# Attention sums with 32-column products only, and a block's end in more steps

## The chip, the cores and the metric

The kernel runs on one core of one Trainium2 chip. The metric is device time in microseconds, from the launch of the one program to its end. TensorE is called PE here, VectorE DVE, ScalarE ACT, GpSimd POOL, SyncE SP.

## The reference, cut to what matters

One layer: graph attention over 4096 nodes with four heads, then a mixture of eight experts, two for each token. `adj` is a 4096 x 4096 int32 matrix of 0 and 1.

```python
h = jnp.einsum('nd,hdk->hnk', x, W)                     # 4 heads of 64 columns
s_col = jnp.einsum('hnk,hk->hn', h, a1)
s_row = jnp.einsum('hnk,hk->hn', h, a2)
e = leaky_relu(s_row[:, :, None] + s_col[:, None, :], 0.2)
e = jnp.where(adj[None] > 0, e, NEG_INF)
h_prime = jnp.einsum('hij,hjk->hik', softmax(e, -1), h)
out = jnp.transpose(h_prime, (1, 0, 2)).reshape(N, 256)
y = elu(out) + x @ Wr + br          # then a layer norm, and the sum with x
...
top_w, top_i = jax.lax.top_k(norm(x) @ Wg + bg, 2)      # 8 experts
out = out + w_dense[:, e:e+1] * (gelu(x @ W1[e] + b1[e]) @ W2[e] + b2[e])
```

All inputs are float32, and so are all products of the attention.

## The kernel before, in words

**Attention.** The adjacency comes transposed. The 4096 output rows are taken in four row blocks `a` of 1024 (`R`), each of two halves of 512 (`B`). For each row block, 32 column blocks `j` of 128 nodes pass by. For one j, DVE makes for each head h a tile `w` of 128 x 1024 weights (both halves) by one instruction (line 1235), from the row factors `er`, the column factor `eb` and the mask `am`. ACT makes the mask out of the int32 adjacency (line 1120), which SP loads. The pool of w has 10 tiles, four for a column block. PE then makes two kinds of products, both with the 512 elements of a w half as the moving operand:

- the rows (`sum_rows`, line 770): `ha` of a head, 64 columns, into `acc[half][h // 2]`, a PSUM bank for two heads. A product covers 64 of the 128 columns of PE's array; the products of heads 1 and 0, and those of heads 3 and 2, lie on different halves of the array and can run at the same time. Eight products for a column block.
- the weights' sums (`sum_weights`, line 779): `unit`, two columns, into two rows of `den` at partition 32 h. A product lies on one of four column groups of 32; the four heads can run at the same time. Eight products for a column block.

A float32 product appears in the profile as two matmuls and two weight loads. `attend` (line 785) makes rows first where j is even and in the last j, and sums first where j is odd, so that equal widths stand next to each other. `queue` (line 408) fixes the order of all these products among themselves. All else is placed between them by a scheduler, which orders the instructions of each engine when the kernel is built.

In the first row block, PE also projects the node features for coming column blocks (`norm_block`, `project_block`); there the first four column blocks are taken half by half.

**A row block's end.** `finish_blocks` (line 942) is a generator. Its first step copies the four accumulators and `den` to SBUF on ACT (lines 949, 952), which frees them for the next row block. Its other steps are run one by one, one after each column block of the next row block (in the last row block two after odd ones). They transpose `den` on PE (line 956) and take the reciprocals `z` on DVE; for each half (`finish_block`) they transpose the sums on PE (line 985, into `ptr`), scale them on ACT (line 987), and do ELU, residual, layer norm and the sum with x on DVE and ACT (lines 994 to 1014). `route_rows` (line 805) then transposes the normalised rows (line 815), multiplies with the router's weights in 32-column products (line 826), transposes the logits back (line 836), picks two experts for each token on DVE (lines 841 to 875), counts places by matmuls with a triangle and with ones (lines 884, 886), and writes the rows into the experts' lists by 16 indirect DMAs on POOL (line 934). For the first row block it also finds tokens that are not in a list (`missed`, `hit`, line 926). Each `yield` is a border between two steps. `ordered[0]` is false in this part and true after the attention.

**After the attention** come the expert tiles (`fetch`, `turn`, `up`, `down`), in an order written out by hand; the last row block's end runs among them (`sums_out`, `turn_sums`, `last_block`).

The general path (`with tc.If(general > 0)`), for scores of a wide spread, is not taken with these inputs.

## Time and profile before

| | us |
|---|---|
| median of 3 runs | 1320.18 |
| the runs | 1319.53 to 1321.72 |
| profiled execution | 1319.03 |
| its span | 1317.4 |
| row block 0 (with projection) | 29.7 to 275.1 |
| row block 1 | 275.1 to 457.7 |
| row block 2 | 457.7 to 639.6 |
| row block 3 | 639.6 to 821.7 |
| expert tiles | 821.7 to the end |

How to read it: the span is the time from the first to the last instruction that the profile shows; the profiled execution's time is 1.6 us longer, and the median of the runs is 1.2 us above that. In a line of a group or a timeline, "128\*64" means a product of 128 rows and 64 columns, "x2048" the number of instructions, "idle before" how long the engine had nothing to do, and "<-" what ended that. PE is the matmuls, PEld the weight loads. A matmul's duration contains its way through the array, so the distance from one start to the next, not the duration, tells the rate.

### The profile page before, as it was taken

The page shows a single profiled execution, that of the slowest core. Times are in us where ns is not written, and L with a number is a line of the kernel's source. Part 1 is how long each engine was busy: PE and PEld are TensorE (multiplying, and loading weights), DVE is VectorE, ACT ScalarE, POOL GpSimd, SP SyncE. Part 2 cuts the span into 40 slices and gives each one's busy share as a digit, 9 for nine tenths or more (in the row PEclk, how much of TensorE's full clock was granted, in tenths as well). Part 3 has the DMA queues.
Part 4 walks back from the last instruction along what each step waited for, and adds up shares of the span by engine and source line. Part 5 has one row for each costly group of instructions (what it writes and reads, how often), then busy time and mean ns, then how long its engine had stood idle before and what let it go on. Part 6 is the DMA issues. An engine that isn't in the chain of part 4 may idle for free.

```text
span 1317.4 us, 19120 instructions
## 1 busy us (share of the span) xinstructions
PE 1281.8 (97%) x7025; PEld 676.9 (51%) x7025; DVE 869.9 (66%) x1746; ACT 444.3 (34%) x888; POOL 226.7 (17%) x190
## 2 busy tenths in 40 slices
PE   7999999999999999999999999999999999999997
PEld 4423344222232222232222322888888877888886
DVE  6899977889999989999899997665111111121110
ACT  4212221135541336421355311533323332323332
POOL 1000010000006000015000150125222222222222
PEclk9999999999999999999999999999999999999999
DMA  7434333344444535535333341987866786878782
GB/s 220 173 97 160 101 108 97 112 149 119 118 128 149 172 90 136 144 101 157 97 112 100 101 153 42 331 265 206 281 164 194 185 185 150 194 207 209 177 213 51
DMA packets 144129, 202.43 MB, mean 154 GB/s; under 512 B 49712, under 2 KB 113856, under 8 KB 143376
## 3 DMA queue, kind: packets, MB, share of 16 engines
q1 hardware_dynamic: 122432, 161.26, 41.3%
q0 software_dynamic: 19360, 32.53, 11.0%
q10 hardware_dynamic: 2224, 7.22, 1.5%
q8 instruction: 60, 0.98, 0.3%
q14 instruction: 53, 0.43, 0.1%
HBM read 171.89 MB, written 29.08 MB: 153 GB/s over the span
## 4 chain that ended last, share of the span: by engine, by line
PE 58%; DVE 9%; issue 2%; ACT 1%; DMA 0%; POOLq 0%; DVEq 0%; ACTq 0%
PE po L1417 18%; PE ph L1386 17%; PE acc L770 14%; PE den L779 7%; DVE w L1235 6%; PE pt L1368 1%; DVE y L1014 0%; DVE y L1008 0%; DVE y L1000 0%; DMA out<-o_last,ids 0%; PE ptr L985 0%; PE pl L826 0%; DVE y L997 0%; PE ptx L815 0%; ACT y L987 0%
## 5 line engine op out<-in xcount | busy, mean ns | idle before, releaser
L1235 DVE SCALAR_TENSOR_TENSOR w<-er,eb,am 128x1024 f32<-128x1024 f32 x496 | 608.9, 1277 | 43.3 <-PE den L779 41.1
L770 PE MATMUL acc<-w,ha 128*64 128x512 f32 x2048 | 464.8, 599 | 7.5 <-DVE w L1235 7.0
L770 PEld LDWEIGHTS acc<-w,ha 128*64 128x64 f32 x2048 | 137.7, 137 | 303.5 <-issue 287.5
L1120 ACT ACTIVATE am<-adj 128x1024 bf16<-128x1024 int32 x124 | 131.1, 1057 | 373.5 <-DVE w L1235 323.0
L779 PE MATMUL den<-w,unit 128*2 128x512 f32 x2048 | 238.4, 594 | 7.5 <-DVE w L1235 7.1
L1386 PE MATMUL ph<-xT,w 128*128 128x256 f32 (+1 forms) x1056 | 240.8, 386 | 1.3 <-DVE xT L1372 0.7
L1417 PE MATMUL po<-w,hT 128*128 128x256 f32 x1088 | 240.3, 379 | 0.0
L1390 ACT ACTIVATE hT<-ph,bias 128x256 f32<-128x256 f32 (+1 forms) x264 | 126.5, 480 | 290.6 <-PE ph L1386 205.0
L1417 PEld LDWEIGHTS po<-w,hT 128*128 128x128 f32 x1088 | 205.5, 190 | 27.7
L1386 PEld LDWEIGHTS ph<-xT,w 128*128 128x128 f32 x1056 | 200.2, 190 | 35.8 <-DVE xT L1372 1.1
L1428 DVE SCALAR_TENSOR_TENSOR o<-po,share,b2s 128x256 f32<-128x256 f32 x66 | 31.8, 482 | 259.1 <-PE po L1417 246.2
L1439 POOL DMA_INDIRECT out<-o,ids x66 | 103.5, 1568 | 330.6 <-DMA out<-o,ids 205.1
L779 PEld LDWEIGHTS den<-w,unit 128*2 128x2 f32 x2048 | 43.9, 84 | 178.1 <-issue 151.7
L934 POOL DMA_INDIRECT lists<-xe,at x64 | 86.0, 1344 | 132.5 <-issue 55.0
L1018 POOL DMA_DIRECT2D out<-y x6 | 4.7, 782 | 335.6 <-issue 166.1
L1372 DVE COPY xT<-pt 128x256 f32<-128x256 f32 x13 | 5.5, 423 | 61.8 <-PE pt L1368 61.8
L188 ACT ACTIVATE m<-y,off 128x256 f32<-128x256 f32 x48 | 23.8, 499 | 23.3 <-DVE off L185 23.3
L1409 ACT ACTIVATE b2s<-b2b,share 128x256 f32<-128x256 f32 x68 | 30.8, 503 | 0.0
L626 PE MATMUL ph<-wall,xT 128*128 128x264 f32 x112 | 30.5, 392 | 0.3 <-DVE sc L636 0.3
L650 PE MATMUL pr<-wr,xT 128*128 128x256 f32 x112 | 29.5, 385 | 0.4 <-ACT xT L609 0.2
L987 ACT ACTIVATE y<-ptr,z 128x64 f32<-128x64 f32 x96 | 22.0, 312 | 15.3 <-PE ptr L985 15.3
L1235 DVE SCALAR_TENSOR_TENSOR w<-er,eb,er 128x512 f32<-128x512 f32 x32 | 22.1, 741 | 5.6 <-issue 5.1
(316 smaller groups left out, 620.0 us busy)
## 6 DMA issues: line engine op xcount, KB each, us to landing
w<-in_L_ffn_W SPq DMA_DIRECT2D x66, 1024.0 KB, 6.3
adj<-in_adj SPq DMA_DIRECT2D x126, 512.0 KB, 3.8
er<-parts ACTq DMA_DIRECT2D x3, 2048.0 KB, 7.7
b2b<-in_L_ffn_b SPq DMA_DIRECT2D x33, 128.0 KB, 3.6
early<-lists SPq DMA_DIRECT2D x16, 260.0 KB, 8.0
residual<-rb POOLq DMA_DIRECT2D x8, 512.0 KB, 3.8
rb<-residual SPq DMA_DIRECT2D x8, 512.0 KB, 4.4
out<-y POOLq DMA_DIRECT2D x8, 512.0 KB, 3.6
```

The source lines that it names most:

```text
L626: nc.tensor.matmul(ph, xT[:, c, ts(t, P)], wall[:, c, :], start=(c == 0), stop=(c == DC - 1),)
L770: queue(nc.tensor.matmul(acc[half][h // 2][ts(h % 2, K), :], ha[:, j, ts(h, K)], w[half][h], start=(j == 0), stop=(j == NT - 1),))
L779: queue(nc.tensor.matmul(den[h * Q : h * Q + HB, :], unit[:, j, h, 1 - half : 1 - half + HB], w[half][h], start=(j == 0 and half == 0), st ...
L934: ins = nc.gpsimd.indirect_dma_start(lists, bass.IndirectOffsetOnAxis(ap=at[:, k, t : t + 1], axis=0), xe[:, t, :], None,).ins
L1120: nc.scalar.activation(am, at, AF.Relu, scale=2.0)
L1235: nc.vector.scalar_tensor_tensor(wh[:, these], er[:, these, h], eb[:, j, h : h + 1], mask[:, these], op0=OP.max, op1=OP.min,)
L1386: order_of(nc.tensor.matmul(ph, job["w1"][:, c, ts(f, P)], xT[:, c, :], start=(c == 0), stop=(c == DC - 1),))
L1390: job["gelu"] = nc.scalar.activation(hT[:, f, :], ph, AF.Gelu, bias=job["bias"][:, f : f + 1]).ins
L1409: nc.scalar.activation(b2s[k], b2b, AF.Identity, scale=share[:, k : k + 1])
L1417: order_of(nc.tensor.matmul(po, hT[:, f, ts(k, CH)], w2[:, f, :], start=(f == 0), stop=(f == FC - 1)))
L1428: given_out.append(nc.vector.scalar_tensor_tensor(o, po, share[:, k : k + 1], b2s[k], op0=OP.mult, op1=OP.add).ins)
L1439: add()
```

## The change: what it does

1. **Every product of the attention lies on 32 columns.** A head's rows are made in two products of 32 columns each (`rows_of_head`), so a column block has 16 products of rows and 8 of sums. The sums of head h lie in `den` at 32 times `PLACE[h]`, where PLACE is (2, 3, 0, 1).
2. **`attend` mixes both kinds.** First the rows of heads 1 and 0, for each half; then for each half the sums of heads 1 and 0 with the rows of head 2; then for each half the rows of head 3 with the sums of heads 3 and 2. Each four in this order fills the four column groups. There is no longer a special order in the last column block.
3. **Two reciprocals for one** (`shares_of`), as heads no longer stand in order in `den`.
4. **More steps in `route_rows`**: before the transposes of the rows, between the router's products and the transposes of the logits, between these and what DVE takes of them, between the counting matmuls and what DVE takes of them; and, for the first row block, before and after the products of `hit`. With `ordered[0]` true the steps are as before.

```diff
+PLACE = (2, 3, 0, 1)
...
-        def sum_rows(w, j, halves):
+        def rows_of_head(w, j, half, h):
+
+            for g in range(K // Q):
+                here = h % 2 * K + g * Q
+                queue(nc.tensor.matmul(
+                    acc[half][h // 2][here : here + Q, :],
+                    ha[:, j, h * K + g * Q : h * K + (g + 1) * Q], w[half][h],
+                    start=(j == 0), stop=(j == NT - 1),
+                ))
+
+        def weights_of_head(w, j, half, h):
+
+            here = PLACE[h] * Q
+            queue(nc.tensor.matmul(
+                den[here : here + HB, :], unit[:, j, h, 1 - half : 1 - half + HB], w[half][h],
+                start=(j == 0 and half == 0), stop=(j == NT - 1 and half == HB - 1),
+            ))
+
+        def attend(w, j, halves):
+
 
             for half in halves:
-                for h in (1, 0, 3, 2):
-                    queue(nc.tensor.matmul(
-                        acc[half][h // 2][ts(h % 2, K), :], ha[:, j, ts(h, K)], w[half][h],
-                        start=(j == 0), stop=(j == NT - 1),
-                    ))
-
-        def sum_weights(w, j, halves):
-
+                for h in (1, 0):
+                    rows_of_head(w, j, half, h)
             for half in halves:
-                for h in reversed(range(H)):
-                    queue(nc.tensor.matmul(
-                        den[h * Q : h * Q + HB, :],
-                        unit[:, j, h, 1 - half : 1 - half + HB], w[half][h],
-                        start=(j == 0 and half == 0), stop=(j == NT - 1 and half == HB - 1),
-                    ))
-
-        def attend(w, j, halves):
-
-
-            rows_first = j % 2 == 0 or j == NT - 1
-            for add in (sum_rows, sum_weights) if rows_first else (sum_weights, sum_rows):
-                add(w, j, halves)
+                for h in (1, 0):
+                    weights_of_head(w, j, half, h)
+                rows_of_head(w, j, half, 2)
+            for half in halves:
+                rows_of_head(w, j, half, 3)
+                for h in (3, 2):
+                    weights_of_head(w, j, half, h)
+
+        def shares_of(pd):
+
+            z = small.tile([P, TB, H, HB], F32, tag="z", name="z")
+            for h in range(0, H, 2):
+                nc.vector.reciprocal(z[:, :, h : h + 2], pd[:, :, PLACE[h] : PLACE[h] + 2, :HB])
+            return z
...
             turned_rows = []
+            if not ordered[0]:
+                yield
             for g in range(0, n, TB):
...
                 nc.scalar.copy(lTs[-1], pl)
-            if ordered[0]:
-                yield
+            yield
             pg = bank([P, n, Q], "pg")
...
+            if not ordered[0]:
+                yield
             full = [P, n, E]
...
+            if not ordered[0]:
+                yield
             rank = small.tile(full, F32, tag="rank", name="rank", bufs=2)
...
+                yield
                 for e in range(E):
...
+                yield
                 nc.vector.tensor_copy(others, po)
...
-            z = small.tile([P, TB, H, HB], F32, tag="z", name="z")
-            nc.vector.reciprocal(z, pd[:, :, :, :HB])
+            z = shares_of(pd)
```

The last replacement is made in `finish_blocks` and in `turn_sums`.

## The prediction

> **What bounds the kernel now.** I read the page first, then busy time by stage, the chain of waits in order of time, the timeline of one steady stretch, and the built order of both kernels. "Column block" means one j; I count them 0 to 127 through the four row blocks (32 each).
>
> ```profile
> PE 1281.8 (97%) x7025; PEld 676.9 (51%) x7025; DVE 869.9 (66%) x1746; ACT 444.3 (34%) x888; POOL 226.7 (17%) x190
> ...
> L770 PE MATMUL acc<-w,ha 128*64 128x512 f32 x2048 | 464.8, 599 | 7.5 <-DVE w L1235 7.0
> ...
> L779 PE MATMUL den<-w,unit 128*2 128x512 f32 x2048 | 238.4, 594 | 7.5 <-DVE w L1235 7.1
> ```
> The attention is 703 us of PE work. Each product is two matmul records (2048 for 1024 products).
>
> ```profile
> core 0: us, PE busy (x) PEld busy (x) DVE busy (x) ACT busy (x) POOL busy (x), PEclk, DMA share, GB/s
> 29.70:275.10 245.40, 238.84 (x1316) 92.30 (x1316) 215.32 (x397) 55.01 (x112) 11.32 (x15) 0.99 0.41 131
> 275.10:457.70 182.60, 179.08 (x1117) 50.71 (x1117) 172.21 (x232) 71.88 (x132) 28.28 (x20) 1.00 0.44 130
> 457.70:639.60 181.90, 178.89 (x1109) 50.70 (x1105) 171.45 (x226) 70.79 (x130) 29.22 (x20) 1.00 0.43 123
> 639.60:821.70 182.10, 178.90 (x1108) 51.66 (x1105) 168.14 (x250) 63.42 (x122) 22.86 (x18) 1.00 0.33 102
> ```
> These are the four row blocks. PE idles 3.0 to 3.5 us in each of the last three, DVE 10 to 14: PE bounds them, with DVE close behind. After 821.7 come the expert tiles, which the change leaves as they are but for one more reciprocal on DVE, busy there for 125 of 495 us.
>
> The chain in a steady stretch, and the same place in the timeline:
> ```profile
> 422.37 7.02 PE acc L770 x32
> 429.39 3.54 PE den L779 x32
> ```
> ```profile
> 428.36 0.14 PEld L770 LDWEIGHTS acc<-w,ha 128*64 128x64 f32 x2 [0.28 <-issue]
> ...
> 429.32 0.11 PEld L779 LDWEIGHTS den<-w,unit 128*2 128x2 f32 x8 [0.81 <-issue]
> ...
> 429.75 0.10 PEld L779 LDWEIGHTS den<-w,unit 128*2 128x2 f32 x4 [0.33 <-issue]
> ...
> 432.86 0.20 PEld L770 LDWEIGHTS acc<-w,ha 128*64 128x64 f32 x4 [0.86 <-issue]
> ```
> A slot (loads of one pass of 2 wide or 4 narrow products) lasts 0.429 us, whether two products of 64 columns run in it or four of 2. Where the width changes, the load comes late (0.81 and 0.86 idle, not 0.3).
>
> **The change, part by part.**
>
> *Width changes, removed.* Two column blocks are 32 matmuls of rows at two a slot and 32 of `den` at four, 16 + 8 slots: 24 x 0.429 = 10.30 us, but the chain has 7.02 + 3.54 = 10.56. The 0.26 are the two width changes. After, a column block is 24 products in six fours, again 12 slots, with no change of width. 120 changes survive beside other work in the trace of before, so 60 pairs x 0.265 = 15.9 us less. The first slot of 64 columns after any whole-array work is about 0.05 longer too (433.35 against 432.86, 0.49, in the same timeline); some 27 such returns: 1.3 us less.
>
> Does a mix of 2 and 32 columns keep the rate? The router's products show it:
> ```profile
> 383.86 0.11 PEld L779 LDWEIGHTS den<-w,unit 128*2 128x2 f32 x4 [0.32 <-issue]
> 384.29 0.13 PEld L826 LDWEIGHTS pl<-xT,wg 128*32 128x32 f32 x4 [0.32 <-issue]
> 384.71 1.06 PE L826 MATMUL pl<-xT,wg 128*32 128x128 f32 x32
> ```
> From 2 to 32 columns costs nothing (384.29 - 383.86 = 0.43, idle 0.32 as inside a stretch). Thirty-two matmuls of 128 elements, four at a time, run 1.06 us with the tail of the last, 0.27: about 0.109 a slot. Four of these are 0.436, 0.007 over 0.429; as 512 elements pay a slot's fixed part once and not four times, I take 0.429 and keep 0.436 as the upper end: 12 x 128 x 0.007 = 10.8 us more. Lower end: 0.429, nothing gained, since the stream itself is as long.
>
> *Instructions.* 2048 matmul records and as many loads more; 96 instructions in a block's 5.15 us, 54 ns each. In the router's burst 64 went out in some 2.4 us after a wait of PE's own sequencer at 383.0, 38 ns each, so I cost the issue at nothing. [...]
>
> *Fours that are cut apart, added.* Each product holds one of four column groups for two slots, 0.858 us. In the built order of before, whole-array transposes stand between whole pairs or fours everywhere. In the changed one many stand after 7 of 24 products (four of the first half, three of the second, then the transposes, then the eighth): seven products take 2 x 0.858, the other 17 take 5 x 0.858, seven turns for six. Counting, between whole-array instructions, the fullest column group against a quarter of the products, I get 6 extra turns in row block 0 (blocks 8 to 23; one more in the start-up, hidden), 3 in the next (36, 42, 43), 4 (67, 68, 74, 75), 5 (98, 99, 103, 104, and 111 to 113): 18 x 0.858 = 15.4 us more. Bounds: 0 if PE waits there anyway, 15.4 if it never does. I take all, as DVE has its idle time just there (2.4 us before 280.6, 2.3 before 303.6).
>
> *PE's waits for DVE.* In odd blocks `den` comes first and needs all four w tiles at once:
> ```profile
> 315.19 1.04 PE L779 MATMUL den<-w,unit 128*2 128x512 f32 x8 [1.02 <-DVE w L1235]
> ...
> 362.42 1.90 PE L779 MATMUL den<-w,unit 128*2 128x512 f32 x16 [1.13 <-DVE w L1235]
> ```
> After, heads 1 and 0 suffice to begin; head 2 is due 1.7 us later, head 3 3.4. Heads 0 and 1 are also given back a third of a block earlier, so DVE gets ahead further. A tile takes DVE 1.20 (chain), four 4.80, under PE's 5.15. Such waits are 2.4 us in row block 1, as much in 2 (the same places), 1.4 in 3; with PE faster some stay: I take 4.5 of 6.2 away, bounds 0 and 6.2. The hit matmuls' wait (0.5 us, once) goes with the new step behind the comparisons: 5.0 together.
>
> *Block's end.* At j = 31 the rows used to come before `den`, which left four slots to empty the accumulators. Now the last rows and `den` end together, and the next block needs `den` empty after four slots, not eight. In the built order of ACT the copy of `den` stands behind one more mask at row blocks 2 and 3:
> ```profile
> 457.90 0.69 ACT L952 ACTIVATE ud<-den,tiny 128x512 f32<-128x512 f32 x1 [0.27 <-PE den L779]
> 460.33 1.06 ACT L1120 ACTIVATE am<-adj 128x1024 bf16<-128x1024 int32 x1 [1.75 <-DVE w L1235]
> ```
> That mask waits for DVE's last w of two blocks on: with h0 and h1 back 1.5 us before the end, two tiles of 1.20 and the mask of 1.06, `den` is copied (0.69) at about 2.9 after the end, where PE wants it at 1.72: 1.2 lost, twice. Queued behind: the next masks, which have a block's lead. Row block 1 loses 0.3 (its copies wait for the sums already). Together 2.6 more; bounds 0 and 4.
>
> *Steps and reciprocals.* Four more steps per row block, six in the first: at one a block they end by block 58, 88 and 114, before the next row block; the list writes on POOL (some 25 us) start up to 18 us later but nobody waits until the first expert tile, whose rows are loaded at 797.6 and used at 821.6. Four more reciprocals of about 0.2 us on DVE, inside its idle 10. Without that cover 0.8.
>
> Sum: -15.9 - 1.3 + 15.4 - 5.0 + 2.6 = -4.2. The profiled execution took 1319.0 (span 1317.4); that gives 1314.8. The median of the runs is 1.2 above it: **1316.0 us**.
>
> **Rivals.**
>
> *The cuts are hidden.* PE would have waited at them for the sums' copies or for w, so half or less of the 15.4 is paid. For it: ACT ends some of PE's waits at the transposes; against it: DVE's idle time at the same places. -4.2 - 7.7: 1308.
>
> *DVE takes over.* PE's gain in row blocks 1 to 3 turns into waiting for w. For it: 172 of 182.6 us busy; against: 4.80 per block against 5.15. Then PE's gains, cuts and ends there all vanish in DVE's time, and row block 0 pays 5.1 for 27 blocks x 0.13 = 3.6: +1.5, or +4.1 if the ends are paid: 1320 to 1324.
>
> *Slower: a slot of four products of 32 columns is longer.* Place: every slot of the attention. At 0.436 (the router's rate), -4.2 + 10.8: 1326.8. It decides from 0.432 on (4.2 / 1536 slots = 0.003). Against it: four `den` products at 0.429; for it: their loads are 84 ns, those of 32 columns 110, and no run of such products longer than 1.1 us is in the trace.
>
> *Not the change it says.* If 2 and 32 columns count as different widths, each mixed four drains, far above 100 us; 384.29 speaks against it.
>
> **How the numbers follow.** 0.2% (2.6 us) is what a measurement can tell from no change. Forecast 0.50 (its own range 1310 to 1321: faster 0.34, same 0.14, slower 0.02); hidden cuts 0.18, all faster; DVE 0.15 (0.02, 0.09, 0.04); longer slot 0.15 and different widths 0.02, slower. Faster 0.54, same 0.23, slower 0.23. From 1307 to 1325 leaves out the low half of the hidden cuts' spread and most of the longer slot: under 2 in 10.
>
> **What would show it.** In the steady stretches no width change: loads four at a time every 0.429 us, 10.30 for two blocks. At the cut places (36, 42, 43, 67 and on) PE's loads come one at a time for two slots, or the block lasts 0.86 longer. PE's waits for w nearly gone. At the starts of row blocks 2 and 3 PE waits for ACT's copy of `den`. I am wrong if the slots are 0.432 or more, if PE's waits for DVE grow, or if the cuts cost much less than 15 us.

## The result and the profile after

The changed kernel takes 1318.38 us (median of 12 runs, 1315.11 to 1324.27); the kernel before, run beside it, 1321.97 (12 runs, 1319.53 to 1326.95). The ratio is 0.9977, 95% interval 0.9960 to 0.9993: 3.6 us less, where 4.2 less were forecast. 1316.0 was predicted, with a range of 1307 to 1325. The fastest runs of the two differ by 4.4 us (1315.11 against 1319.53).

The profiled execution took 1322.95 us (span 1321.3), which is at the slow end of the 12 and 3.9 more than the profile before. The expert tiles are 7.4 longer in it, 503.1 us against 495.7, for nearly the same instructions (see the last section). The four row blocks, which the change is about, took 787.6 us against 792.0: 4.4 less. From here on I compare these four lengths. They repeat to a few tenths where the order and the granted clock are the same (row block 3 took 182.1 us in the kernel before and in e5, 183.8 in the kernel after and in e4); with 1.7 us more at a lower clock, e10 took 185.1 there (see the table below).

From the page of the kernel after, the engines' busy times and the two groups of products:
```profile
PE 1283.2 (97%) x9072; PEld 699.7 (53%) x9073; DVE 872.2 (66%) x1750; ACT 443.2 (34%) x888; POOL 241.1 (18%) x190
...
L771 PE MATMUL acc<-w,ha 128*32 128x512 f32 x4096 | 679.0, 596 | 7.1 <-DVE w L1255 7.1
...
L780 PE MATMUL den<-w,unit 128*2 128x512 f32 x2048 | 527.0, 593 | 2.1 <-ACT ud L974 2.1
```
The wait of the sums (`den`) for w, 7.1 us before, is gone; a wait for the copy of `den`, 2.1, is new. The two busy times overlap now (products of both kinds run side by side), so their sum means nothing.

Busy time by row block in the kernel after (columns: length, then busy time and instructions of each engine, PE's granted clock, DMA share, GB/s):
```profile
core 0: us, PE busy (x) PEld busy (x) DVE busy (x) ACT busy (x) POOL busy (x), PEclk, DMA share, GB/s
30.55:278.43 247.88, 239.89 (x1828) 98.12 (x1828) 218.21 (x397) 55.98 (x113) 11.33 (x15) 0.99 0.41 128
278.43:455.24 176.81, 176.22 (x1628) 54.79 (x1631) 169.60 (x231) 69.46 (x130) 36.03 (x20) 1.00 0.44 131
455.24:634.37 179.13, 177.34 (x1619) 55.29 (x1615) 171.34 (x229) 70.23 (x131) 30.41 (x20) 1.00 0.45 130
634.37:818.18 183.81, 179.42 (x1620) 57.74 (x1613) 166.77 (x250) 63.64 (x124) 28.02 (x18) 1.00 0.34 101
```
Length minus PE's busy time is PE's idle time. Summed over the four, PE's work fell from 775.7 to 772.9 us and its idle time from 16.3 to 14.8. By row block the gain is +2.5, -5.8, -2.8, +1.7: row blocks 1 and 2 pay for 0 and 3.

PE's loads in a steady stretch of the kernel after (start, busy, idle before):
```profile
290.12 0.13 PEld L771 LDWEIGHTS acc<-w,ha 128*32 128x32 f32 x4 [0.30 <-issue]
290.55 0.09 PEld L780 LDWEIGHTS den<-w,unit 128*2 128x2 f32 x2 [0.30 <-issue]
290.56 0.12 PEld L771 LDWEIGHTS acc<-w,ha 128*32 128x32 f32 x2
290.98 0.09 PEld L780 LDWEIGHTS den<-w,unit 128*2 128x2 f32 x2 [0.30 <-issue]
290.99 0.12 PEld L771 LDWEIGHTS acc<-w,ha 128*32 128x32 f32 x2
```
Four loads every 0.43 us, two of 2 columns and two of 32, with no late load where the width changes. A column block without other work lasts 5.15 us in the trace (10.30 for two; before 10.56).

A place where transposes cut a four, column block 67:
```profile
473.31 0.16 PEld L771 LDWEIGHTS acc<-w,ha 128*32 128x32 f32 x8 [0.17 <-issue]
473.77 0.12 PEld L771 LDWEIGHTS acc<-w,ha 128*32 128x32 f32 x3 [0.30 <-issue]
474.20 0.12 PEld L771 LDWEIGHTS acc<-w,ha 128*32 128x32 f32 x3 [0.31 <-issue]
475.81 0.20 PEld L1006 LDWEIGHTS ptr<-ident,u 128*128 128x128 f32 x2 [1.49 <-ACT y L1008]
476.18 0.11 PEld L771 LDWEIGHTS acc<-w,ha 128*32 128x32 f32 x1 [0.17 <-issue]
```
Four products (two passes each, x8), then three in a turn made for four, then the transposes, then the eighth product.

### The profile page after: what moved, and what is told of

Same layout as the page of the kernel before. It is cut to its first block, busy times and chain, and to the rows that moved or that the text cites. A ratio compares the mean times of both kernels' runs of the same rounds, so it can differ in the third digit from the quotient of the medians.

```text
span 1321.3 us, 23213 instructions
## 1 busy us (share of the span) xinstructions
PE 1283.2 (97%) x9072; PEld 699.7 (53%) x9073; DVE 872.2 (66%) x1750; ACT 443.2 (34%) x888; POOL 241.1 (18%) x190
## 4 chain that ended last, share of the span: by engine, by line
PE 42%; DVE 7%; issue 1%; ACT 0%; DMA 0%; POOLq 0%; DVEq 0%; ACTq 0%
PE ph L1406 17%; PE po L1437 17%; PE acc L771 5%; DVE w L1255 4%; PE den L780 3%; PE pt L1388 1%; DMA out<-o_last,ids 0%; DVE y L1035 0%; DVE y L1029 0%; DVE y L1021 0%; PE pl L843 0%; POOLq L1561 0%; ACT xe L814 0%; DVE y L1100 0%; DVE y L1018 0%
## 5 line engine op out<-in xcount | busy, mean ns | idle before, releaser
L771 PE MATMUL acc<-w,ha 128*32 128x512 f32 x4096 | 679.0, 596 | 7.1 <-DVE w L1255 7.1
L780 PE MATMUL den<-w,unit 128*2 128x512 f32 x2048 | 527.0, 593 | 2.1 <-ACT ud L974 2.1
L771 PEld LDWEIGHTS acc<-w,ha 128*32 128x32 f32 x4096 | 190.4, 110 | 302.4 <-issue 286.1
L1406 PE MATMUL ph<-xT,w 128*128 128x256 f32 (+1 forms) x1056 | 244.0, 389 | 5.6 <-DVE xT L1392 4.7
L1448 DVE SCALAR_TENSOR_TENSOR o<-po,share,b2s 128x256 f32<-128x256 f32 x66 | 31.8, 483 | 257.4 <-PE po L1437 237.1
L780 PEld LDWEIGHTS den<-w,unit 128*2 128x2 f32 x2048 | 99.1, 85 | 150.9 <-issue 146.6
L956 POOL DMA_INDIRECT lists<-xe,at x64 | 100.2, 1566 | 151.6 <-issue 53.6
L651 PEld LDWEIGHTS pr<-wr,xT 128*128 128x128 f32 x112 | 20.7, 190 | 8.0 <-issue 2.7
```

The source lines that it names most:

```text
L651: nc.tensor.matmul(pr[:, t % 2, :], xT[:, c, ts(t, P)], wr[:, c, :], start=(c == 0), stop=(c == DC - 1),)
L771: queue(nc.tensor.matmul(acc[half][h // 2][here : here + Q, :], ha[:, j, h * K + g * Q : h * K + (g + 1) * Q], w[half][h], start=(j == 0), ...
L780: queue(nc.tensor.matmul(den[here : here + HB, :], unit[:, j, h, 1 - half : 1 - half + HB], w[half][h], start=(j == 0 and half == 0), stop ...
L956: ins = nc.gpsimd.indirect_dma_start(lists, bass.IndirectOffsetOnAxis(ap=at[:, k, t : t + 1], axis=0), xe[:, t, :], None,).ins
L1406: order_of(nc.tensor.matmul(ph, job["w1"][:, c, ts(f, P)], xT[:, c, :], start=(c == 0), stop=(c == DC - 1),))
L1448: given_out.append(nc.vector.scalar_tensor_tensor(o, po, share[:, k : k + 1], b2s[k], op0=OP.mult, op1=OP.add).ins)
```

## The experiments

One table first, so that the parts can be set against each other. Lengths of the row blocks (from the first product of one to the first of the next), PE's work (its busy time) and idle time summed over the four, and the ratio to the kernel before, run on the same chip, with its 95% interval. The granted clock is the share of its full speed that PE is given. "Clock" is the part of PE's work that a lower granted clock made: an estimate, half of the time that PE was busy while the granted clock stood at 0.50 in that run's trace. It goes by the kernel after, where the loads of two neighbouring slots come 0.86 us apart at 0.50 (166.07 and 166.93) and 0.43 at 1.00.

| kernel | row blocks 0, 1, 2, 3 (us) | sum | PE's work | clock | PE idle | ratio to before |
|---|---|---|---|---|---|---|
| before | 245.4, 182.6, 181.9, 182.1 | 792.0 | 775.7 | 2.6 | 16.3 | |
| after | 247.9, 176.8, 179.1, 183.8 | 787.6 | 772.9 | 3.5 | 14.8 | 0.9977 (0.9960 to 0.9993) |
| e4 after without the steps | 248.4, 182.3, 183.5, 183.8 | 798.0 | 778.0 | 3.6 | 19.9 | 1.0071 (1.0054 to 1.0088) |
| e5 before with the steps | 245.1, 181.2, 181.3, 182.1 | 789.8 | 775.3 | 3.0 | 14.5 | 0.9987 (0.9965 to 1.0009) |
| e3 after, old order | 247.0, 181.5, 181.4, 185.6 | 795.4 | 774.8 | 2.7 | 20.6 | 1.0032 (1.0017 to 1.0046) |
| e8 before, rows first always | 250.5, 183.9, 183.0, 184.6 | 802.0 | 793.1 | 3.9 | 8.9 | 1.0072 (1.0050 to 1.0093) |
| e1 transposes between whole blocks | 246.4, 191.6, 194.2, 194.9 | 827.2 | 777.8 | 18.4 | 49.4 | 1.0295 (1.0278 to 1.0312) |
| e9 all between whole blocks | 244.3, 191.5, 193.8, 192.2 | 821.8 | 773.4 | 19.5 | 48.4 | 1.0234 (1.0217 to 1.0251) |
| e10 transposes after 8 | 246.7, 176.4, 178.9, 185.1 | 787.1 | 767.8 | 3.2 | 19.3 | 0.9984 (0.9964 to 1.0005) |
| e14 the same, nine w tiles | 247.0, 175.8, 176.3, 184.0 | 783.1 | 766.0 | 1.7 | 17.2 | 0.9969 (0.9947 to 0.9992) |
| e13 the same, nine w, five masks | 253.1, 176.9, 176.0, 184.0 | 790.0 | 769.1 | 4.7 | 20.8 | 1.0008 (0.9988 to 1.0029) |
| e6 after, den first at the end | 249.1, 177.6, 178.2, 184.4 | 789.4 | 776.7 | 6.3 | 12.8 | 0.9971 (0.9948 to 0.9993) |
| e12 all placings | 244.0, 176.4, 178.0, 184.4 | 782.8 | 764.7 | 5.0 | 18.2 | 0.9922 (0.9896 to 0.9948) |
| e15 the same, nine w, five masks | 254.5, 177.1, 175.5, 185.6 | 792.7 | 768.5 | 9.9 | 24.3 | 0.9988 (0.9966 to 1.0010) |

The clock column matters for what follows. Between 40 and 1300 us the granted clock is 1.00 throughout in the kernel before. In the kernel after it is 1.00 but for two stretches at 0.50: 3.4 us from 163.9 on, after a pause of PE of 1.9 us that ended at 162.9, and 6.8 us from 918.2 on, which begin in a pause of 3.9. Not every such pause has one: PE waits 1.8 us before 724.2 in the kernel after too, and the granted clock stays at 1.00 there.

### The widths: is it the width change or the order?

My theory: 0.265 us for each pair of width changes. The rival: the new order, not the widths, made the block shorter. Two runs, one from each side.

```diff
# e3: 32-column products, in the order of the kernel before
-            for half in halves:
-                for h in (1, 0):
-                    rows_of_head(w, j, half, h)
-            ...
+            rows_first = j % 2 == 0 or j == NT - 1
+            for add in (sum_rows, sum_weights) if rows_first else (sum_weights, sum_rows):
+                add(w, j, halves)
```


> The changed kernel with products of 32 columns, but in the order of the kernel before: all rows of a column block, then all of den, and the other way round in odd blocks. This keeps the equal widths and gives up the new order. 20 extra turns are left in the built order, as in the changed kernel (6, 4, 4, 6 by row block against 8, 3, 4, 5). Theory (the width changes are what the steady block lost, the order is worth only PE's waits for w): two steady blocks still last 10.30 us; the waits for w of odd blocks come back, 4.5 us; the wait at the ends of row blocks 0 to 2 for the copy of den goes, since den is wanted only after all rows, 2.6 us; 1318.4 + 4.5 - 2.6 = 1320.3. Rival (the order, with its pairs of den between rows, made the block shorter): two steady blocks go back to about 10.56 us, some 16 us more, 1336. Rival (2 columns after 32 do cost a width change): between the two, by 0.13 a change.

Steady column blocks last 5.15 us here too, in pairs of 10.30: equal widths alone do it. So the first rival falls, and the second (2 after 32 columns costs a change) as well. The whole came out higher than either value of the theory: 1323.9 on a chip where the kernel before took 1318.7. The waits for w at the sums of odd blocks came back, 8.4 us by the page of e3 (7.1 in the kernel before, none after), more than the 4.5 that I had put down; PE's idle time is 20.6 us against 14.8 of the changed kernel. So the order is worth more beside the faster products than I had it; that this is because DVE's rate stayed while PE's rose fits, but is argued.

```diff
# e8: the kernel before, twice as many width changes
-            rows_first = j % 2 == 0 or j == NT - 1
+            rows_first = True
```


> The kernel before with the rows ahead of den in every column block, not only in the even ones: the width changes twice in every block, not once; 263 changes in the built order against 139, so 62 pairs more. Theory (a pair costs 0.265 us): 16.4 us more; less what is saved of PE's waits for w of odd blocks, at most 6.2, and 2.6 more for 3 cut groups of four: 10 to 19 us more than before, two steady blocks 10.83 us against 10.56. Rival (the change of width is free and the 10.56 have another cause, such as the end of each stretch of rows): two steady blocks stay at 10.56 and the whole within 3 us of before.

PE's loads in a steady stretch of e8:
```profile
609.63 0.10 PEld L779 LDWEIGHTS den<-w,unit 128*2 128x2 f32 x4 [0.32 <-issue]
610.60 0.20 PEld L770 LDWEIGHTS acc<-w,ha 128*64 128x64 f32 x4 [0.86 <-DVE w L1235]
...
613.23 0.14 PEld L770 LDWEIGHTS acc<-w,ha 128*64 128x64 f32 x2 [0.29 <-issue]
614.18 0.11 PEld L779 LDWEIGHTS den<-w,unit 128*2 128x2 f32 x8 [0.81 <-issue]
...
616.01 0.20 PEld L770 LDWEIGHTS acc<-w,ha 128*64 128x64 f32 x4 [0.86 <-DVE w L1235]
```
Both late loads stand in every block now; a block lasts 616.01 - 610.60 = 5.41, and 5.41 - 5.15 = 0.26 is the price of the pair, as forecast. Over the four row blocks PE's work is 17.4 us more (793.1 - 775.7); of this 2.6 are three cut turns, 1.3 the clock and 13.5 the 62 pairs, 0.22 each. The time rose by 10.0 only, since PE's idle time fell by 7.4: rows first needs one w tile to begin, not four, and the waits of `den` for w (7.1) are gone in e8.

### The steps: what are they worth?

The prediction put them at nothing. The rival: they are what keeps PE from waiting in the router's part.

```diff
# e4: the changed kernel without the added yields (one of six shown)
             turned_rows = []
-            if not ordered[0]:
-                yield
             for g in range(0, n, TB):
```


> The changed kernel without its added steps in the router's part (the yields), so with the 32-column products, their order, and the split reciprocals alone. Theory (steps cost and bring nothing but the hit matmuls' wait of 0.5): 23 extra turns in the built order against 20 (8, 5, 5, 5), so 3 x 0.858 = 2.6 more, and 0.5 more for the hit matmuls: 1318.4 + 3.1 = 1321.5, row block 1 about 2 us longer than 176.8, row block 2 about 1 longer than 179.1. Rival (the steps are what kept PE from waiting: each transposed result then has a column block's time to be worked on): PE's waits in the router's part, under 0.3 us in row blocks 1 and 2 of the changed kernel, grow to 1 us or more each, row blocks 1 to 3 longer by 3 us each, 1328. Rival (the steps do harm in the last row block, where the two waits of 1.9 and 1.2 us stand in the changed kernel): row block 3 shorter than 183.8 by 2 us or more.

PE's waits over row blocks 1 and 2, first of e4, then of the kernel after:
```profile
PE ptx L830 <- ACT xe L814: 3.1, 8, 1.1
PE pg L851 <- ACT lT L846: 2.5, 2, 1.3
PE ptr L999 <- ACT y L1001: 1.2, 2, 0.6
PE po L941 <- DVE hit L935: 0.4, 1, 0.4
```
```profile
PE den L780 <- ACT ud L974: 1.2, 1, 1.2
PE ptr L1006 <- ACT y L1008: 1.2, 2, 0.6
```
(Columns: who waits for whom, us in all, times, longest.) Without the steps PE waits 3.1 us for the normalised rows `xe` and 2.5 for the router's logits `lT`, both of ACT. With them these two are gone in row blocks 1 and 2. The changed kernel is 10.4 us shorter over the four row blocks than e4, 5.5 in row block 1 and 4.4 in 2, half of it idle time and half PE's work (778.0 - 772.9 = 5.1, of which three turns explain 2.6; the rest is open). The ratios say the same: 1.0071 against 0.9977, some 12 us. So the rival "the steps are what kept PE from waiting" is right in row blocks 1 and 2, with more than the 3 us each that it named; in row block 3 it is wrong, and so is the third rival, harm there: 183.8 in both kernels.

```diff
# e5: the kernel before with the added yields
             turned_rows = []
+            if not ordered[0]:
+                yield
```


> The kernel before with the added steps of the router's part and of the comparison of hits alone; products, order and reciprocals as before. Against the 1318.7 to 1322 of the kernel before. Theory of the prediction (the steps move work without a cost, and save only the wait of the hit matmuls, 0.5 us): the same within 1 us. Theory after the run without them (the steps give ACT a column block's time for the normalised rows and the router's logits, so PE does not wait there): that took 10 us off the 32-column kernel; in the kernel before PE waits for neither at the router's transposes in the trace, so the steps by themselves bring under 2 us, and their 10 us are a repair of what the new order did to the router's part. Rival (the steps are a gain of their own, whatever the products): 5 us or more less than before.

2.2 us less over the row blocks, and a ratio that can't be told from 1. So the steps have little worth of their own. The products alone make the kernel slower (+6.0 over the row blocks, ratio 1.0071), the steps alone hardly change it, and together they are faster: the steps repair what the products' order did to the router's part. Why that part waits with the new order and not with the old wasn't traced to one instruction; what is shown is that it does and for whom.

### The cuts: are they paid?

The theory: each whole-array instruction behind 7 of 24 products costs a turn of 0.858 us. The rivals: the turn is hidden behind a wait, or DVE takes over. (The count used here, 20 turns in the changed kernel, adds up partial fours over each stretch and takes in the start-up; the prediction's 18 left that out.)

```diff
# e1: the transposes of the sums in the order of the products
-                    nc.tensor.transpose(pt[:, t % 2, ts(i, P)], u[:, i, ts(t, P)], ident)
+                    queue(nc.tensor.transpose(
+                        pt[:, t % 2, ts(i, P)], u[:, i, ts(t, P)], ident
+                    ))
```


> The changed kernel with the finishing blocks' transposes of the sums (ptr) written into PE's queue between two whole column blocks, not after 7 of 24 products; nothing else. In the built order this takes away 10 of the 12 extra turns of row blocks 1 to 3 (3, 4 and 3); the 8 in row block 0 and 2 in row block 3 stay. Theory (a cut costs a turn of 0.858 us, and nothing hides it): row blocks 1, 2, 3 go from 176.8, 179.1, 183.8 to about 174.2, 175.7, 181.2; 8.6 us in all, from the 1318.4 median of the changed kernel to about 1309.8. Rival (cuts hidden: PE would have waited there anyway): the waits for the sums' copies or for w come in the turns' place, row blocks within 1 us each of what they were, 1317 to 1319. Second rival (DVE takes over as soon as PE gains): waits for w grow in row blocks 1 to 3, half of the 8.6 or less comes through, 1314 or more.

1356.8 us where the kernel before took 1318.7: 38 more, and outside every value that I had put down. The group of these transposes in e1's page:
```profile
L1006 PE MATMUL ptr<-ident,u 128*128 128x128 f32 x48 | 11.2, 318 | 31.8 <-ACT y L1010 31.8
```
PE's idle time rose by 34.6 us, 31.8 of them here. Two pairs of transposes share a bank, and the second pair waits until ACT has scaled the first (`y`). In the changed kernel the seven products between the pairs, two turns of 0.858, cover most of that (its waits for `y` are 1.7 us); side by side nothing covers it. So the order that cuts a four does something.

The pauses cost more than themselves. After them the granted clock stood at 0.50, nine times in row blocks 1 to 3 of e1 and never there in the changed kernel. Two neighbouring stretches (busy time by stretches, as above):
```profile
294.60:298.00 3.40, 3.40 (x20) 0.85 (x16) 0.00 (x0) 0.86 (x4) 0.00 (x0) 0.50 0.38 130
298.00:304.80 6.80, 4.37 (x40) 1.29 (x36) 4.87 (x4) 1.92 (x6) 0.00 (x0) 1.00 0.04 12
```
By the estimate of the table this is 17.1 us of PE's work in row blocks 1 to 3 (over the whole run the mean granted clock is 0.983 in e1, 0.992 in the changed kernel). Without it PE's work there is 173.1, 173.2 and 176.3 us, against 176.2, 177.3 and 179.4 in the changed kernel: 10.4 less, for ten turns that the theory puts at 8.6. So the turns did go, and the waits and the clock hid it.

> The changed kernel with three things: the finishing blocks' transposes between whole column blocks; the transposes and projections of row block 0 too, a quarter of them behind each column block; and the last column block of a row block with its den products ahead of the rows of heads 2 and 3, den copied behind the sums of heads 0 and 1. Of the 20 extra turns 3 are left (1 in the start-up, 2 in row block 3). Theory (all of them are paid, and the copy of den is awaited for some 2.4 us): 17 x 0.858 + 2.4 = 17.0 less than 1318.4: 1301.4, and down to 1296 if PE's waits in row block 0 (1.0, 1.4, 1.9 and 1.4 us at column blocks 8, 12, 15 and 16 of the changed kernel) go with the new places. Rival (DVE takes over): tiles of w at 1.20 us and DVE's other work give a row block about 171 us of DVE, so row blocks 1 and 2 cannot fall under some 172 to 174, and with waits for w at PE the whole ends at 1307 or more. Rival (the new places in row block 0 make PE wait, for the normalised rows above all): row block 0 longer than 247.9.

```diff
# e9, beside e1's edit: row block 0 in quarters, den ahead of the last rows
+                        if a == 0 and j % TB == 0:
+                            n = j // TB
+                            todo = chain(
+                                project_steps(n + 1, True, queue) if n + 1 < NB else (),
+                                norm_steps(n + 2, measured(n + 2), queue) if n + 2 < NB else (),
+                            )
                         attend(weigh(er, load_mask(a, j), j, both), j, both)
+                        if a == 0:
+                            next(todo, None)
```
1349.3, for the same reason: 31.6 us of waits for `y`, and 19.5 at the lower clock. Row block 0 went from 247.9 to 244.3, with PE's work 5.7 us less (239.9 to 234.2; seven turns are 6.0) and its idle time 2.1 more, most of that in the start-up, where the projections now come later. The rival of a longer row block 0 falls.

Next the test that changes one thing. Seven products and eight both take two turns, so the second pair may stand behind eight at no delay (where nobody waits, the next transpose starts 1.85 us after the first of seven in the changed kernel, 480.96 to 482.81, and 1.86 after the first of eight in e14, 470.23 to 472.09):

```diff
# e10, row blocks 1 and 2 only
             for half in halves:
                 for h in (1, 0):
                     rows_of_head(w, j, half, h)
+            if held_turn:
+                held_turn.pop()()
```
Here `held_turn` holds the second pair of transposes and its scalings, put there by `finish_block`.

> The changed kernel with the second of each two pairs of transposes of the sums (ptr) put into PE's queue after 8 of a column block's 24 products, not after 7; only for the transposes that stand in row blocks 1 and 2, so that row blocks 0 and 3 are a control. Seven products and eight both take two turns of the four column groups, so PE reaches the transposes at the same time and ACT has as long as before for the values it owes; only the lone eighth product behind them goes. In the built order all 3 + 4 extra turns of row blocks 1 and 2 are gone, and ACT's order in row block 2 is that of the changed kernel. Theory (a cut costs the lone turn of 0.858 us, paid in full): row block 2 from 179.1 to 175.7, row block 1 from 176.8 to 174.2, together 6.0; the others within 0.5 us; 1318.4 - 6.0 = 1312.4. Rival (the turn was hidden, since PE waits for ACT there in any case, as it did for 32 us when all transposes stood between whole blocks): the wait takes its place, row blocks 1 and 2 within 1 us, 1317 to 1319. Rival (DVE takes over): waits for w of 1 us and more appear in row blocks 1 and 2, half comes through, 1315.

PE's work fell by three quarters of what the theory has: 176.2 to 174.4 in row block 1 (three turns are 2.6) and 177.3 to 174.6 in 2 (four are 3.4). Where nobody waits, the price of a turn stands alone: in e10 and e14 alike, column block 73 falls from 6.49 to 5.66 us and column block 81 from 7.14 to 6.31, 0.83 each, with the same instructions in it. (They show too that a turn need not be paid at the cut: the cuts are in blocks 68 and 75, the column groups run on out of step at 5.15 us a block, and the turn comes ahead of the next whole-array instruction. In the changed kernel the last run of `den` before the transposes at the end of block 73 is four matmuls in 1.45 us, from 511.96 on; at an even place it is two in 0.60, from 294.00 on, 0.85 less.) But the row blocks themselves are 0.4 and 0.3 us shorter only. The time went into waits for `y` (1.7 us three times before, 4.3 in eight times now) and for the copy of `den` (2.1 to 3.1). The first rival had it right for this kernel. (Row blocks 0 and 3, left as they were, moved by -1.2 and +1.3, more than these two: the first has 2.1 us less of the lower clock, the second 1.7 more.) What the wait is made of shows in ACT's timeline of e10 at column blocks 66 to 67:
```profile
465.80 1.06 ACT L1155 ACTIVATE am<-adj 128x1024 bf16<-128x1024 int32 x1 [4.09 <-DVE w L1270]
471.70 1.06 ACT L1155 ACTIVATE am<-adj 128x1024 bf16<-128x1024 int32 x1 [4.84 <-DVE w L1270]
472.67 0.91 ACT L1016 ACTIVATE y<-ptr,z 128x64 f32<-128x64 f32 x4
```
The first pair of transposes was issued at 470.8 to 470.9; their scalings stand in ACT's queue behind a mask of 1.06 us, and that mask waits until 471.70 for DVE to finish with an older w. PE waits for ACT, ACT for DVE, and DVE for the tiles that PE gives back (3.8 us in two waits over column blocks 67 to 75).

Is it the mask's tile or DVE itself? Five mask tiles let the masks run two blocks further ahead; they need the room of a w tile, so the control has nine w tiles alone.

```diff
# e14 (and e13), both on e10
-                        wh = work.tile([P, HB, B], F32, tag="w", name="w", bufs=10)
+                        wh = work.tile([P, HB, B], F32, tag="w", name="w", bufs=9)
# e13 in addition
-            am = gat.tile([P, R], BF16, tag="am", name="am", bufs=3)
+            am = gat.tile([P, R], BF16, tag="am", name="am", bufs=5)
```


> The kernel with the transposes after 8 products, and five tiles for ACT's masks (am) in the place of three, so that a mask may be made two column blocks earlier; to make room, nine tiles for w in the place of ten, and one w tile in the branch that this data never enters. Theory (what took the place of the cut turns is a ring: PE's transposes wait for ACT's values y, which stand in ACT's queue behind a mask, which waits for a tile that DVE's w of three blocks back must give up, and DVE waits for PE): the waits for y fall from 4.3 us to under 1.5 and those for the copy of den from 3.1 to under 1, row blocks 1 and 2 from 176.4 and 178.9 to about 175 and 176; some 5 us off the whole. Rival (DVE is full: 172.2 of row block 2's 178.9 us busy, so PE cannot run further ahead whatever ACT does): the same waits stand before w, row blocks 1 and 2 within 1 us. The ninth w tile is a confound, told apart by the next kernel.

> The kernel with the transposes after 8 products, with nine tiles for w in the place of ten and nothing else: the control for the run with five mask tiles, with DVE a tile (1.2 us) less ahead of PE. Theory (the ring): DVE's w come later where it was ahead, so the waits for y and for w are as long or longer, row blocks 1 and 2 the same to 2 us longer than 176.4 and 178.9. Rival (the tenth tile is idle): all within 0.5 us.

The control surprised: nine tiles gave row block 2 in 176.3 us, 2.5 less than ten. Five masks added next to nothing to that (row block 2 176.0 against 176.3, row block 1 176.9 against 175.8 with 1.5 of clock in it) and cost 6 us in row block 0, nearly all in column block 1, where PE waits 5.5 us for the projected rows of DVE (1.3 in e14). So the theory that the mask's tile is the bottleneck falls. But why did nine tiles help? PE's built order around the transposes is the same in e10 and e14 to the product; ACT's is not. ACT's timeline of e14 at the same place:
```profile
466.10 1.06 ACT L1155 ACTIVATE am<-adj 128x1024 bf16<-128x1024 int32 x1 [3.88 <-DVE w L1270]
470.34 0.93 ACT L1016 ACTIVATE y<-ptr,z 128x64 f32<-128x64 f32 x4 [3.19 <-PE ptr L1012]
472.00 1.06 ACT L1155 ACTIVATE am<-adj 128x1024 bf16<-128x1024 int32 x1 [0.74 <-ACT y L1016]
```
The scheduler, with other numbers of tiles, placed the first scalings ahead of the mask. They start as soon as the transposes are done, and PE doesn't wait. Column blocks 66 to 68 take 17.5 us in e14 (5.66 + 6.16 + 5.65), 19.0 in the changed kernel (5.66 + 7.65 + 5.67) and 18.7 in e10. Of the 1.5 between e14 and the changed kernel, all in block 67, 0.64 is the wait for `y` and 0.85 the turn of the cut there; the turn of the cut in 68 is the one that stands in 73. At column block 74, where the scalings stand behind another mask, e14 waits 2.0 us, more than a turn is worth. Against e10, column blocks 67 and 68 are 1.3 shorter and 74 is 1.3 longer: the places of the scalings give and take the same.

Most of the 2.5 us is the first column block of row block 2, 7.57 us in e10 and 5.63 in e14. PE waits there for the copy of `den` (`ud`), 2.24 us in e10 and 0.30 in e14. First ACT and PE at that place in e10, then ACT in e14:
```profile
454.48 1.06 ACT L1155 ACTIVATE am<-adj 128x1024 bf16<-128x1024 int32 x1 [1.52 <-DVE w L1270]
455.44 0.67 ACT L976 ACTIVATE ud<-den,tiny 128x512 f32<-128x512 f32 x1
456.17 0.60 PE L780 MATMUL den<-w,unit 128*2 128x512 f32 x2 [2.24 <-ACT ud L976]
```
```profile
454.53 0.69 ACT L976 ACTIVATE ud<-den,tiny 128x512 f32<-128x512 f32 x1
456.37 1.06 ACT L1155 ACTIVATE am<-adj 128x1024 bf16<-128x1024 int32 x1 [1.16 <-issue]
```
In e10 the copy stands behind a mask that waits for DVE; in e14 that mask comes after it.

Row block 2 as a whole, e10 and e14:
```profile
452.03:630.90 178.87, 174.63 (x1619) 55.45 (x1615) 172.23 (x229) 70.24 (x131) 34.73 (x21) 1.00 0.44 131
```
```profile
453.07:629.40 176.33, 174.01 (x1619) 55.54 (x1615) 171.96 (x229) 71.36 (x132) 32.56 (x21) 1.00 0.45 134
```
DVE is busy for 172.0 of 176.3 us in e14. That DVE were full at 178.9 (the rival in e13) is refuted by this, but 4.4 us is all that is left to it.

### A block's end

```diff
# e6
+            if j == NT - 1:
+                for half in halves:
+                    for h in (1, 0):
+                        rows_of_head(w, j, half, h)
+                for half in halves:
+                    for h in (1, 0, 3, 2):
+                        weights_of_head(w, j, half, h)
+                for half in halves:
+                    for h in (2, 3):
+                        rows_of_head(w, j, half, h)
+                return
...
-            for half in range(HB):
-                for i in range(H // 2):
+            for i in range(H // 2):
+                for half in range(HB):
                     nc.scalar.activation(u[:, half, i], acc[half][i], ...)
-            nc.scalar.activation(ud, den, AF.Identity, bias=tiny)
+                if i == 0:
+                    nc.scalar.activation(ud, den, AF.Identity, bias=tiny)
```


> The changed kernel with one thing: in the last column block of a row block, den's products stand ahead of the rows of heads 2 and 3, and ACT copies den behind the sums of heads 0 and 1. Theory (the block's end costs the wait for the copy of den, 1.4 us at the start of row block 2 and 1.0 at that of 3): in ACT's built order that copy is still behind a mask at row block 2 and no longer at row block 3, so 1.0 to 2.0 us off, row block 3 the most. Rival (the copies of the sums of heads 2 and 3 are then the late ones): the wait for them takes its place, within 0.5 us. The cuts are as in the changed kernel but for one more in row block 1 (0.86 us).

PE's waits from 278 to 760 us, in the kernel after and in e6:
```profile
PE den L780 <- ACT ud L974: 2.1, 2, 1.2
PE ptx L832 <- ACT xe L814: 1.9, 2, 1.8
PE ptr L1006 <- ACT y L1008: 1.7, 3, 0.6
PE pk L902 <- DVE on L899: 1.0, 1, 1.0
```
```profile
PE ptx L843 <- ACT xe L825: 1.9, 2, 1.8
PE ptr L1018 <- ACT y L1020: 1.5, 3, 0.6
PE acc L771 <- ACT u L982: 1.2, 1, 1.2
PE pk L913 <- DVE on L910: 1.0, 1, 1.0
```
The wait for `ud` is gone in both places; the first column block of row block 2 went from 6.54 to 5.15 us, that of row block 3 from 6.19 to 5.15, together 2.4. As the rival had it, the copies of the sums are the late ones once, 1.2 us, but at the start of row block 1, where the transposes of `den` had waited before. Row blocks 0, 1 and 3 are 0.6 to 1.2 longer each: row block 1 by the one more cut (PE's work 0.8 more), 0 and 3 beside 1.0 and 1.7 us more at the lower clock. So the whole is the same (0.9971 against 0.9977). The price of the wait is shown; that the fix pays is not.

### Together

> The changed kernel with the transposes of the sums after 8 products in row blocks 1 and 2, the projections and transposes of row block 0 between whole column blocks (a quarter behind each), and den's products ahead of the rows of heads 2 and 3 in the last column block of a row block. 6 extra turns are left of 20 (1 in the start-up, 5 in row block 3). Theory (turns paid, waits as in the parts' own runs): row block 0 at 244.3 as when this was tried with the other placing, -3.6; row blocks 1 and 2 at 174.2 and 175.7, -6.0; the waits for the copy of den down from 2.1 to 1, -1; row block 3 as it is, 183: 1318.4 - 10.6 = 1307.8. Rival (DVE takes over once PE gains so much): 1312 or more, with waits for w in row blocks 1 and 2.

e12 has e10's placing, e9's row block 0 and e6's end. 1312.9 us where the kernel before took 1321.5 on that chip, ratio 0.9922 (0.9896 to 0.9948): faster than both kernels, against the changed one by about 0.55% (0.9922 / 0.9977). 10.6 us off the changed kernel were forecast; the row blocks lost 4.8 (787.6 to 782.8), nearly all in row block 0 (-3.9). Without the clock's part PE's work fell by 9.7 (14 turns are 12.0), but its idle time rose by 3.4, of which 2.1 in row blocks 1 and 2 for the reason that e10 showed, and the clock's part rose by 1.5 in all, by 1.7 in row block 3. No waits for w appeared in row blocks 1 and 2, so it isn't DVE that takes the rest directly; the waits for `y` are 4.2 us, as in e10.

> The kernel with all placings mended (transposes after 8 products in row blocks 1 and 2, row block 0's projections between whole column blocks, den's products ahead of the last rows), and five mask tiles and nine w tiles. Theory (the ring): a further 3 to 5 us less than the 782.8 us that the four row blocks took with three mask tiles, most of it in row blocks 1 and 2; about 0.989 of the kernel before. Rival (DVE full, or the ninth w tile missed): within 1 us of 782.8, 0.992.

792.7 in place of 782.8: 10.4 us lost in row block 0, 9.1 of them in column block 1 of the start-up, and row blocks 1 and 2 as in e13. The theory fell here as there. e12 with nine w tiles and three masks, which e14 suggests, wasn't run.

## Why the prediction was right, and where only its sum was

The forecast was -4.2 us; the runs show -3.6 and the row blocks -4.4. Its two kinds of terms hold up as well: PE's own work, -15.9 - 1.3 + 15.4 = -1.8 forecast, -2.8 in the trace; PE's waits, -5.0 + 2.6 = -2.4 forecast, -1.5 in the trace. The -2.8 hold a part that the sum has no term for: 0.9 us more at the lower clock, so that PE's work without it fell by 3.8, twice the forecast. That the whole came out within a few tenths is in part luck, as the steps below show. Step by step:

- **Width changes removed** (-15.9 and -1.3): right in size. Steady blocks last 5.15 us as forecast, also with the old order (e3), and a pair of changes costs 0.26 in a steady block of e8, 0.22 over all of e8's 62. The slot of four mixed products is 0.429 us, not 0.436 as in the router's short products; so the rivals "longer slot" and "2 and 32 columns count as different widths" are out.
- **Instructions** (0): right. 96 instructions go out in 5.15 us, and the block lasts no longer than its 12 slots (12 x 0.429 = 5.15): issuing them shows no cost there.
- **Fours cut apart** (+15.4): right as PE's work. Take the seven turns of row block 0 away and PE's work falls by 6.1, 5.8 without the clock's part (e12; 6.0 by the count); the seven of row blocks 1 and 2, by 4.5 (e10; 6.0 by the count) and 5.6 (e14). One turn by itself is 0.83 (column blocks 73 and 81). The cuts stand where the prediction put them, but those in 68 and 75 don't lengthen their own blocks, as its signs had it; their turns come in 73 and 81. The rival "the cuts are hidden" is wrong for the kernel as it is, where PE does that work with hardly an idle moment (0.6 and 1.8 us in row blocks 1 and 2), but right for anyone who takes them away: in e10 a wait for ACT came in their place at once.
- **PE's waits for DVE** (-5.0): the waits for w went, as forecast (7.1 us at the sums before, none after). But e4, with the new order and no steps, has 19.9 us of PE's idle time against 16.3 before: without the steps waits for ACT in the router's part take the place of the waits for w, and more. The step as the prediction put it, "5.0 together", holds only with the next one.
- **Steps and reciprocals** (0): this is the step that failed. They are worth 10.4 us in the row blocks beside the new products. I costed them by what they move (list writes on POOL, later ends) and looked for nobody waiting; I didn't ask what the transposes and the logits would wait for without them, once the products' order had changed. The missing loss of the products alone (+6.0, where the prediction's terms give about -1 with three more cuts) and the missing gain of the steps cancelled, so the sum was right through two errors of opposite sign: that is luck.
- **Block's end** (+2.6): right in mechanism and size for row blocks 2 and 3: forecast 1.2 twice, measured 1.39 and 1.04 by what e6 took away. (The terms that the prediction names, two tiles, a mask and the copy from 1.5 us ahead of the end, add up to 2.65 and not 2.9, so 0.9 twice would have followed from them.) The 0.3 at row block 1 was short: the column block before it went from 7.63 to 8.68 us, with PE's transposes of `den` waiting 1.6 for the same copy.
- **DVE takes over**: not in this kernel. DVE idles 7.2 and 7.8 us in row blocks 1 and 2 after the change, and no wait for w stands there. It is near: with e14's 176.3 only 4.4 are left.

## What to carry to other kernels

When products share the array by column groups, count whole-array instructions between them in the built order: each that stands where the groups are unevenly filled can cost one lone turn of PE's work, as it did here (0.83 us in column blocks 73 and 81, where nobody waits). But before moving such an instruction, look for what the products ahead of it cover: here they covered ACT's answer, and moving the transposes together cost 32 us of waits, and some 17 more through the lower clock that followed these waits. And price an added step border by what would wait without it, in the kernel as the rest of the change leaves it; "it only moves work" was worth 10 us, and a cause tested alone on the kernel before would have shown almost none of it.

## What the runs showed that was not expected

- **The expert tiles, the same but for one reciprocal, take 495.7 to 503.6 us.** In the fourteen profiles of the table that stretch took 495.7 in five (the kernel before, e1, e3, e4, e9), and 497.6 to 503.6 in the other nine. The kernel after is one of the long ones. Two stretches of 20 us in it, and the same place in the kernel before:
```profile
898.00:918.00 20.00, 17.41 (x86) 14.60 (x84) 12.77 (x93) 4.65 (x11) 12.54 (x12) 1.00 0.85 239
918.00:938.00 20.00, 18.35 (x75) 15.72 (x76) 4.70 (x24) 5.34 (x12) 6.05 (x9) 0.83 0.89 291
```
```profile
902.00:922.00 20.00, 20.00 (x100) 17.54 (x100) 14.07 (x107) 6.60 (x15) 10.19 (x10) 1.00 0.79 227
```
  PE idles 4.2 us there, 3.9 of them in one pause. The granted clock is 0.50 for the 6.8 us from 918.2 on, 0.83 over the second stretch of 20 us, with 75 matmuls in place of about 99. By the estimate of the table this pause of 4 us so cost some 7. PE waits there for DVE's copies, and DVE's queue was held before that; what held it is open and wasn't tried. Without the 7.4 us this profile would have taken 1315.5, near the fastest run (1315.11); that the spread of the other runs has the same cause is likely, but not shown. It is why the row blocks were compared.
- **Products of 2 and of 32 columns mix without a cost that shows**: four of 32, or two of 32 with two of 2, take a slot of 0.429 us in the steady blocks (5.15 / 12), the same as two of 64 columns, while 64 next to 2 columns costs 0.26 for there and back.
- **A smaller pool made the kernel faster**: nine w tiles in place of ten (e14), through other places in ACT's queue, that of the copy of `den` above all (1.9 of 2.5 us in row block 2); that the tile itself does nothing wasn't tried apart from that order.
